# Four edits to the order of row gathers, neighbour lists and first-graph copies in a graph-network kernel on one core

## The chip, the core and the metric

The kernel runs on one core of one Trainium2 chip, in one launch. The core has five engines, each with its own instruction stream worked through in order: TensorE (PE in the profile, its weight loads PEld), VectorE (DVE), ScalarE (ACT), GpSimd (POOL) and SyncE (SP). SP here only issues DMAs; GpSimd mostly issues gathers by index, called indirect DMAs. The metric is the device time of the launch in microseconds (us), less is better.

## The reference

Sixteen graphs of 1024 nodes with 64 channels each, and a symmetric weighted adjacency matrix of 1024 x 1024 per graph. Four layers follow one another; each normalises the rows of x, applies a relu to give h, and adds a result to x:

```
layer 0: x += tanh([h, adj @ h] @ W1 + b1) @ W2 + b2
layer 1: x += ((adj + I) @ h) / rowsum(adj + I)
layer 2: x += relu((h + quantiles(h)) @ W1 + b1) @ W2 + b2, times the node mask
layer 3: x += (adj @ h / degree) @ Wn + h @ Ws + bias
```

The quantiles of layer 2 set the shape of the kernel. For each node the neighbours are those with a positive entry, thinned out by a rule on their rank (every k-th neighbour of a node with more than 10 is removed, in both directions), and the node itself. Over the remaining neighbours, channel by channel, the reference sorts the values of h and takes the 0.25, 0.5 and 0.75 quantiles with linear interpolation, weighted 0.25, 0.5, 0.25.

## The kernel before, in words

Nodes of a graph are dealt by falling number of neighbours to 8 blocks of 128, one node per partition. Blocks are sorted in five groups, `GROUPS`: block 0 alone, block 1 alone, and the pairs 2-3, 4-5, 6-7. `PLACES` says how many neighbours a block's nodes may have at most in its columns (21, 19, 17, 16, 15, 13, 12, 11), and `LISTS` how many are listed (40, 24, 24 and five times 16). The few nodes of block 0 with more than 21 neighbours have the surplus fetched as packed rows (`PACKS`).

Six Python generators (streams) each run over the graphs and emit the instructions of one kind of work:

- `adjacency`: loads the matrix two blocks at a time (`load_rows`, on SP), makes a 0/1 form `nb` (L947, VectorE), transposes by TensorE (L954) into `adjt` with PSUM copies on ScalarE (L955), finds removed neighbours `gone` (L978-L1011), writes per node a row of neighbour codes `keys_d` to DRAM (relu at L1032, a Sign for the count at L1035, both ScalarE), and ranks the nodes (L1055 to L1081).
- `layers`: layers 0 and 1 and the h of layer 2, stored to DRAM as `h_d` (L1236).
- `neighbour_lists`: per block one gather of key rows on GpSimd (`load_keys`, L1096, four buffers, so the load for block i+4 follows block i), then VectorE's MAX8 takes eight neighbours a round (L1111, L1125, L1127) into `found`. After the eighth block three operations turn all 168 columns into row numbers, `index` (L1135 to L1137). Then the numbers of the packed rows go to DRAM and back as `pack` through seven SP transfers (L1141, L1143), and the quantile weights are made.
- `gathers`: per graph three packed gathers (L1264), then group by group, place by place, one gather of 128 rows of `h_d` into `raw` per block (L1283), 124 in all. A group's `raw` has one buffer, so group k of graph b is emitted after the sort of group k of graph b-1. The packed rows travel through DRAM into `raw` by SP (L1273, L1276).
- `sorts`: compare-and-exchange steps on VectorE over `raw` and `other` (L1316) and the weighted sum (L1333, L1335).
- `tail`: gathers the results back by node (L1355), ends layer 2 and computes layer 3.

The order is set by a planner that runs while the program is built. Each stream yields the time at which it wants to go on, by a model clock `clk` (`clk.dve`, `clk.pool`, ...). The loop at the end of `direct_path` always takes the first stream in the list that is due, adjacency first, sorts last; when none is due, the clock jumps. `done` holds what has been emitted, and `over_graphs` holds a stream back until what it needs is there: gathers need `("index", b)` and `("layers", b)`. A gate (L919 to L925) ties GpSimd to this order: VectorE clears a mark, and GpSimd copies it before the gathers behind it, so they can't start before VectorE has come to this place. Gates stand at least 3 us of the model clock apart.

Of the kernel before, what the change touches and what calls it, by code (L numbers as in the profile page):

```python
# [7 lines left out]
F32 = mybir.dt.float32  # L8
F16 = mybir.dt.float16
BF = mybir.dt.bfloat16  # L10
I32 = mybir.dt.int32
U16 = mybir.dt.uint16
U8 = mybir.dt.uint8
AF = mybir.ActivationFunctionType
ALU = mybir.AluOpType
AX = mybir.AxisListType

P = 128
# [38 lines left out]
PACKS, NPACK = [(0, 0, 21, 2, 64), (1, 0, 23, 1, 32), (1, 32, 24, 4, 24), (2, 0, 28, 10, 12)], 3  # L57

LISTS = [40, 24, 24, 16, 16, 16, 16, 16]
KB = 4  # L60


# [669 lines left out]
def direct_path(ctx: ExitStack, tc: tile.TileContext, t: dict, out: bass.AP, flag):  # L732
# [207 lines left out]
    def adjacency(b):  # L940
# [4 lines left out]
        for i in range(NB):  # L945
            a = queued.pop(0)
            ts(nb[:, i, :], a, 0.0, None, op0=ALU.is_gt)  # L947
            d = slice(i * P, (i + 1) * P)
            tt(nb[:, i, d], nb[:, i, d], offdiag, ALU.mult)
            for q in range(2):  # L950
                p = bank()
                for u in range(4):
                    j = 4 * q + u
                    nc.tensor.transpose(p[:, u * P:(u + 1) * P], a[:, j * P:(j + 1) * P], identf)  # L954
                nc.scalar.copy(adjt[:, 4 * q:4 * q + 4, i * P:(i + 1) * P],  # L955
                               p.rearrange("p (u m) -> p u m", m=P))
            if i % 2:
                load_rows((NB * b + i) // 2 + 2)
            for q in range(2):
                s = slice(q * 512, (q + 1) * 512)  # L960
                act(nb[:, i, s], nb[:, i, s], AF.Copy, accum_out=mn[:, q, i:i + 1])  # L961
            yield max(after(0.9, pe=2.2, act=2.9) - 3.0, clk.dve + 3.1)
# [55 lines left out]
        for i in range(NB):  # L1018

            p = bank2()  # L1020
            for q in range(2):
                s = slice(q * 512, (q + 1) * 512)
                nc.tensor.matmul(p[:, s], big_i, nb[:, i, s], start=True, stop=False)
                nc.tensor.matmul(p[:, s], big_i, gone[:, i, s], start=False, stop=False)
                nc.tensor.matmul(p[:, s], onerow, jrow[:, s], start=False, stop=False)
                for j in range(4 * q, 4 * q + 4):
                    d = slice(j * P, (j + 1) * P)
                    nc.tensor.matmul(p[:, d], gone[:, j, i * P:(i + 1) * P], big_i, start=False,  # L1028
                                     stop=j == 4 * q + 3 and i // 4 != q)
                if i // 4 == q:  # L1030
                    nc.tensor.matmul(p[:, i * P:(i + 1) * P], identh, big_i, start=False, stop=True)
            act(nb[:, i, :], p, AF.Relu)  # L1032
            if i % 2:
                nc.sync.dma_start(keys_d[(i - 1) * P:(i + 1) * P].rearrange("(u p) n -> p u n", p=P), nb[:, i - 1:i + 1])
            act(p, p, AF.Sign, accum_out=ms[:, i:i + 1])  # L1035
            yield after(0, pe=4.5, act=2.3) - 4.0
# [50 lines left out]
    def neighbour_lists(b):  # L1087
# [13 lines left out]
        gate()  # L1101
        for i in range(KB):
            load_keys(i)
        total = sum(LISTS)
        found = lists.tile([P, total], F32, name="found", bufs=1)
        m = g["m"]
        o = 0
        for i in range(NB):
            src, at = ks[i]
            yield at  # L1110
            nc.vector.max(out=found[:, o:o + 8], in_=src)  # L1111
            clk.dve += 1.15
            yield clk.dve
            less, before = src.bitcast(I16), None
            for r in range(1, LISTS[i] // 8):


                least = found[:, o + 7:o + 8]
                if r == 1:
                    ts(less, src, least, None, op0=ALU.subtract)  # L1120
                else:
                    ts(less, less, before, least, op0=ALU.add, op1=ALU.subtract)
                before = least
                most = nodes.tile([P, 8], U16, name="most")
                nc.vector.max(out=most, in_=less.bitcast(U16))  # L1125
                o += 8
                ts(found[:, o:o + 8], most.bitcast(I16), 0.0, least, op0=ALU.min, op1=ALU.add)  # L1127
                clk.dve += 1.8
                yield clk.dve
            o += 8  # L1130
            load_keys(i + KB)
        index = lists.tile([P, total], I32, name="index")
        to, of = (v.rearrange("p (s u) -> p u s", u=2) for v in (index, found))
        none = lists.tile([P, total // 2], F32, tag="far", name="none", bufs=1)
        nc.vector.tensor_copy(to[:, 1], of[:, 1])  # L1135
        ts(none, of[:, 0], 0.0, float(N + 1), op0=ALU.is_equal, op1=ALU.mult)
        tt(to[:, 0], none, of[:, 0], ALU.add)  # L1137
        pack_d = dram.tile([NPACK, P], I32, name="pack_d")
        pack = nodes.tile([P, NPACK], I32, name="pack")
        for l, p0, s0, ns, nn in PACKS:  # L1140
            nc.sync.dma_start(pack_d[l, p0:p0 + ns * nn].rearrange("(n s) -> n s", s=ns), index[:nn, s0:s0 + ns])  # L1141
        for l, size in enumerate(sizes):
            nc.sync.dma_start(pack[:size, l:l + 1], pack_d[l, :size].rearrange("(n o) -> n o", o=1))  # L1143

        s = nodes.tile([P, 2, NB], F32, name="s")
        tt(s[:, 0], m, cap8, ALU.is_gt)
# [21 lines left out]
        act(far, far, AF.Abs)  # L1168
        for k, w in enumerate((0.25, 0.5, 0.25)):
            act(far[:, k], far[:, k], AF.Relu, bias=wcol[:, k:k + 1], scale=-w)  # L1170
        g.update(index=index, pack=pack)
        done.add(("index", b))
        yield after(1.7, act=1.7)
        while b >= 2 and ("sorts", b - 2) not in done:
            yield None
# [70 lines left out]

    def gathers(b):
        g = state[b]
        yield max(g["rows_at"], clk.pool)
        for k, (b0, n, cap, *_) in enumerate(GROUPS):  # L1250
            while not (b == 0 or ("sort", b - 1, k) in done):
                yield None
            raw = raws.tile([P, cap, n * C], F32, name=f"raw{k}")
            clk.pool = max(clk.pool, clk.dve)
            for i in range(n):
                for s in (PLACES[b0 + i], PLACES[b0 + i] + 1):
                    if s < cap:
                        z = raw[:, s:cap:2, i * C:(i + 1) * C]
                        nc.scalar.copy(z, none[:, s % 2:s % 2 + 1, None].to_broadcast([P, (cap - s + 1) // 2, C]))
                        clk.act = max(clk.act, clk.dve) + 0.2 + (cap - s + 1) // 2 * C / 1400  # L1260
            if k == 0:
                packed = nodes.tile([P, NPACK * C], F32, name="packed", bufs=1)
                for l, size in enumerate(sizes):
                    nc.gpsimd.indirect_dma_start(packed[:size, l * C:(l + 1) * C], None, h_ds[b % 3],  # L1264
                                                 bass.IndirectOffsetOnAxis(ap=g["pack"][:size, l:l + 1], axis=0))
                    clk.pool += 1.39
                rows_d = dram.tile([NPACK, P, C], F32, name="rows_d")
            for s in range(cap):
                if s % (4 // n) == 0:
                    gate()  # L1270
                if k == 0 and s == 9:
                    for l, size in enumerate(sizes):
                        nc.sync.dma_start(rows_d[l, :size], packed[:size, l * C:(l + 1) * C])  # L1273
                if k == 0 and s == 17:
                    for l, p0, s0, ns, nn in PACKS:
                        nc.sync.dma_start(raw[:nn, s0:s0 + ns, :],  # L1276
                                          rows_d[l, p0:p0 + ns * nn].rearrange("(n s) c -> n s c", s=ns))
                for i in range(n):
                    if s >= PLACES[b0 + i]:
                        continue  # L1280
                    clk.pool += 1.39
                    at = sum(LISTS[:b0 + i]) + s
                    nc.gpsimd.indirect_dma_start(raw[:, s, i * C:(i + 1) * C], None, h_ds[b % 3],  # L1283
                                                 bass.IndirectOffsetOnAxis(ap=g["index"][:, at:at + 1], axis=0))
                if (s + 1) % (4 // n) == 0:
                    yield clk.pool - 5
            g[f"raw{k}"] = (raw, clk.pool + 4)
            done.add(("gather", b, k))
        done.add(("gathers", b))
# [125 lines left out]
    nc.vector.memset(none[:, :1], BIG)  # L1415
    nc.vector.memset(none[:, 1:], 0.0)
    sizes = [max(p0 + ns * nn for l, p0, _, ns, nn in PACKS if l == k) for k in range(NPACK)]
    programs = [_program(*group[2:]) for group in GROUPS]
    edge = lists.tile([1, 2, C], F32, tag="ab", name="edge")
    nc.vector.memset(edge[:, 0], 0.0)  # L1420
# [6 lines left out]
    def over_graphs(step, *needs):  # L1427
# [7 lines left out]
        over_graphs(adjacency, ("adjt", 1), ("keys", 1), ("sorts", 3)),  # L1435
        over_graphs(layers, ("rows", 0), ("tail", 3)),
        over_graphs(tail, ("sorts", 0)),
        over_graphs(gathers, ("index", 0), ("layers", 0)),
        over_graphs(neighbour_lists, ("keys", 0), ("gathers", 2), ("sorts", 3)),
        over_graphs(sorts, ("lists", 0)),  # L1440
    ]
# [148 lines left out]
```

## Time and profile before

| what | value |
|---|---|
| median of 3 runs | 3667.72 us (3661.44 to 3670.98) |
| the profiled execution, its own time | 3892.48 us |
| its span, first to last instruction | 3890.7 us |
| granted TensorE clock in it | 0.679 |
| busy: VectorE / GpSimd / TensorE / ScalarE | 78% / 68% / 52% / 37% |
| row gathers L1283 | 1984, 1085 ns each, 532.6 us of issue gaps before them |

The profiled execution is slower than the runs without a profile, so durations from it add up to its own 3892 us and not to the median. A row of the profile names line, engine, operation and tiles (written<-read), the number of instructions, their busy time and mean duration, and after the second bar the engine's idle time before them with what ended it. "issue" is a gap for which the profile shows no cause; behind GpSimd's DMA instructions it is about 0.3 us each time. In a timeline the first two columns are start and duration in us.

### The profile page before, as it was taken

To read this page: it belongs to the slowest core of one execution; us is meant where nothing else is said; L and a number is where in the kernel's file an instruction comes from. 1 tells how busy PE (TensorE), PEld (TensorE's weight loads), DVE (VectorE), ACT (ScalarE), POOL (GpSimd) and SP (SyncE) were. 2 spreads that over 40 slices of the span, in tenths; PEclk is the share of its full clock that TensorE was granted. 3 is DMA by queue.
4 is the path that set the end of the run, shared out by engine and by line. 5 is a ranking of instruction groups with operands and counts; after the bars stand their busy time and mean duration, and the time that the engine had idled before them with its cause. 6 is when DMAs were issued, how large, how long until landed. Compare 5 with 4: busy or idle time off the path is not lost.

```text
span 3890.7 us, 30892 instructions
## 1 busy us (share of the span) xinstructions
PE 2010.3 (52%) x7587; PEld 934.0 (24%) x7587; DVE 3040.5 (78%) x7345; ACT 1424.2 (37%) x2786; POOL 2650.6 (68%) x2792
## 2 busy tenths in 40 slices
PE   6463463746554474645546565565457545641113
PEld 3222221223222222222222222232222212220101
DVE  2557877969787897888788798989699867979572
ACT  5444343244443434333342444343444424330000
POOL 1077565867767776776767677777778776777781
PEclk8676666667676686666666676767667666765555
DMA  2313233152423425233341525242343424232121
GB/s 89 124 40 117 48 98 114 47 166 53 153 64 94 121 65 152 69 114 79 86 126 48 172 54 163 58 156 56 100 119 108 113 52 126 65 105 59 43 52 55
DMA packets 237343, 362.37 MB, mean 93 GB/s; under 512 B 126848, under 2 KB 128496, under 8 KB 237152
## 3 DMA queue, kind: packets, MB, share of 16 engines
q1 hardware_dynamic: 156912, 255.00, 19.0%
q0 software_dynamic: 80096, 104.70, 13.5%
q8 instruction: 62, 1.02, 0.1%
q14 instruction: 129, 1.06, 0.1%
q10 hardware_dynamic: 144, 0.59, 0.0%
HBM read 245.30 MB, written 114.81 MB: 93 GB/s over the span
## 4 chain that ended last, share of the span: by engine, by line
DVE 42%; issue 16%; POOL 10%; PE 10%; another core or an unknown queue 9%; ACT 9%; DMA 4%; SPq 0%; DVEq 0%; ACTq 0%; POOLq 0%
DVE other L1316 11%; DVE raw L1316 10%; POOL raw L1283 8%; DVE most L1125 5%; PE pt L882 4%; DVE found L1111 2%; DVE agg L1335 2%; ACT adjt L1220 2%; ACT sink L1055 2%; DVE k L1120 1%; DMA k<-keys_d,node 1%; POOL res L1355 1%; PE pt L906 1%; DVE nb L947 1%
## 5 line engine op out<-in xcount | busy, mean ns | idle before, releaser
L1283 POOL DMA_INDIRECT raw<-h_d,index x1984 | 2151.8, 1085 | 558.9 <-issue 532.6
L1316 DVE TENSOR_TENSOR other<-raw 128x512 f32<-128x512 f32 (+11 forms) x816 | 536.8, 688 | 152.0 <-DMA raw<-h_d,index 103.6
L882 PE MATMUL pt<-adjt,ha 128*65 128x512 f32 (+1 forms) x1024 | 489.7, 640 | 63.0 <-DVE ha L1207 27.1
L924 POOL COPY gate<-mark 1x1 f32<-1x1 f32 x477 | 162.7, 341 | 409.4 <-DVE mark L922 372.6
L994 PE MATMUL pt<-eh,nbt 128*128 128x512 f16 (+3 forms) x1024 | 238.3, 381 | 322.1 <-ACT nbt L983 256.1
L954 PE MATMUL pt<-ef,a 128*128 128x128 f32 x1024 | 212.5, 367 | 294.9 <-issue 112.4
L1316 DVE TENSOR_TENSOR raw<-other 128x512 f32<-128x512 f32 (+10 forms) x464 | 355.8, 791 | 5.3
L1125 DVE MAX8 most<-k 128x8 uint16<-128x1024 uint16 x208 | 255.4, 1228 | 10.9 <-DVE k L1120 3.3
L954 PEld LDWEIGHTS pt<-ef,a 128*128 128x128 f32 x1024 | 163.4, 190 | 383.8 <-issue 186.6
L1032 ACT ACTIVATE nb<-pt 128x1024 f16<-128x1024 f32 x128 | 130.6, 1021 | 328.7 <-remote 169.3
L955 ACT COPY adjt<-pt 128x512 f32<-128x512 f32 x256 | 140.3, 585 | 282.6 <-remote 148.0
L882 PEld LDWEIGHTS pt<-adjt,ha 128*65 128x65 f32 (+1 forms) x1024 | 149.2, 149 | 386.3 <-issue 375.3
L1028 PE MATMUL pt<-eh,gone 128*128 128x128 f16 x1024 | 128.7, 255 | 181.9 <-DVE gone L1006 90.6
L1316 DVE TENSOR_TENSOR raw<-other,raw 128x640 f32<-128x640 f32 (+3 forms) x448 | 216.5, 494 | 6.7 <-remote 1.8
L994 PEld LDWEIGHTS <-nbt 128*128 128x128 f16 x1024 | 111.2, 121 | 452.8 <-ACT nbt L983 286.0
L1316 DVE TENSOR_TENSOR raw<-raw,other 128x128 f32<-128x128 f32 (+7 forms) x496 | 211.6, 436 | 6.1
L883 ACT COPY big<-pt 64x1024 f32<-64x1024 f32 (+1 forms) x32 | 32.2, 1008 | 502.5 <-PE pt L882 299.3
L961 ACT ACTIVATE nb<-nb 128x512 f16<-128x512 f16 x256 | 159.7, 629 | 147.7 <-DVE nb L947 53.8
L1392 PE MATMUL tm<-at,ha 128*64 128x512 f32 x512 | 176.8, 794 | 67.0 <-DMA at<-adjt_d 59.1
L1316 DVE TENSOR_TENSOR other<-other,raw 128x128 f32<-128x128 f32 (+4 forms) x448 | 201.6, 461 | 4.5 <-DVE other L1316 0.3
L1001 ACT ACTIVATE gone<-pt,sf 128x512 f16<-128x512 f32 x256 | 161.6, 685 | 104.7 <-remote 35.1
L1111 DVE MAX8 found<-k 128x8 f32<-128x1024 f16 x128 | 156.4, 1222 | 42.5 <-DMA k<-keys_d,node 42.4
(189 smaller groups left out, 4249.3 us busy)
## 6 DMA issues: line engine op xcount, KB each, us to landing
a<-in_adj_dram SPq DMA_DIRECT2D x64, 1024.0 KB
adjt_d<-adjt SPq DMA_DIRECT2D x64, 1024.0 KB
at<-adjt_d SPq DMA_DIRECT2D x128, 512.0 KB
keys_d<-nb SPq DMA_DIRECT2D x64, 512.0 KB
raw<-h_d,index POOLq DMA_INDIRECT x1984
x<-in_x_dram SPq DMA_DIRECT2D x16, 256.0 KB
h_d<-h SPq DMA_DIRECT2D x16, 256.0 KB
agg_d<-agg SPq DMA_DIRECT2D x16, 256.0 KB
```

Of the source, the lines that this page charges most:

```text
L882: nc.tensor.matmul(p[p0:p0 + n, s], h[:, j, :n], adjt[:, j, s], start=j == 0, stop=j == NB - 1)
L924: nc.gpsimd.tensor_copy(opened[:, k % 2:k % 2 + 1], slots[:, k % 8:k % 8 + 1])
L954: nc.tensor.transpose(p[:, u * P:(u + 1) * P], a[:, j * P:(j + 1) * P], identf)
L955: nc.scalar.copy(adjt[:, 4 * q:4 * q + 4, i * P:(i + 1) * P], p.rearrange("p (u m) -> p u m", m=P))
L961: act(nb[:, i, s], nb[:, i, s], AF.Copy, accum_out=mn[:, q, i:i + 1])
L994: nc.tensor.matmul(p[:, o:e], nbt[:, j, :], stair[:, :e - o], start=j % 4 == 0, stop=j % 4 == 3 and j != i)
L1001: act(gone[:, i, s], p[:, s], AF.Abs, bias=sf[:, 2 + q, i:i + 1], scale=2.0)
L1111: nc.vector.max(out=found[:, o:o + 8], in_=src)
L1125: nc.vector.max(out=most, in_=less.bitcast(U16))
L1283: nc.gpsimd.indirect_dma_start(raw[:, s, i * C:(i + 1) * C], None, h_ds[b % 3], bass.IndirectOffsetOnAxis(ap=g["index"][:, at:at + 1], axi ...
L1316: tt(view(two[to], *((i, vi) if greater else (j, vj)), w), view(two[s], i, vi, w), view(two[u], j, vj, w), ALU.max if greater else ALU.min)
L1392: nc.tensor.matmul(p[q * C:(q + 1) * C, :], ha[:, j, :], even(ats[j], q), start=j == 0, stop=j == NB - 1)
```

## The change

Block by block, the change does this:

- `found` becomes one constant tile of 176 columns, cleared once, for all graphs. The lists of paired blocks are interleaved in it column by column (`FIRST` has the first column of each group), so that one view covers the group.
- As soon as the last block of a group has its list, three operations make that group's row numbers, and `("index", b, k)` is set; the three at the end go. `gathers` waits for group k's numbers before group k, no longer for all of them.
- The packed numbers go to DRAM and back after block 0 instead of after block 7. The packed gathers move from before the first place to place 4, their way out to DRAM from place 9 to 11.
- `gathers` sets no gate at places past the last gathered one (only group 0 has a whole stretch of those, 21 to 37).
- In graph 0 the second PSUM copy of each block's transposes (128x512) and the relu of L1032 (128x1024) run on VectorE; in the other graphs they stay on ScalarE.

```diff
--- before.py
+++ after.py
@@ -57,6 +57,7 @@
 PACKS, NPACK = [(0, 0, 21, 2, 64), (1, 0, 23, 1, 32), (1, 32, 24, 4, 24), (2, 0, 28, 10, 12)], 3
 
 LISTS = [40, 24, 24, 16, 16, 16, 16, 16]
+FIRST = [0, 40, 64, 112, 144, 176]
 KB = 4
 
 
@@ -952,8 +953,8 @@
                 for u in range(4):
                     j = 4 * q + u
                     nc.tensor.transpose(p[:, u * P:(u + 1) * P], a[:, j * P:(j + 1) * P], identf)
-                nc.scalar.copy(adjt[:, 4 * q:4 * q + 4, i * P:(i + 1) * P],
-                               p.rearrange("p (u m) -> p u m", m=P))
+                copy = nc.vector.tensor_copy if b == 0 and q else nc.scalar.copy
+                copy(adjt[:, 4 * q:4 * q + 4, i * P:(i + 1) * P], p.rearrange("p (u m) -> p u m", m=P))
             if i % 2:
                 load_rows((NB * b + i) // 2 + 2)
             for q in range(2):
@@ -1029,7 +1030,10 @@
                                      stop=j == 4 * q + 3 and i // 4 != q)
                 if i // 4 == q:
                     nc.tensor.matmul(p[:, i * P:(i + 1) * P], identh, big_i, start=False, stop=True)
-            act(nb[:, i, :], p, AF.Relu)
+            if b:
+                act(nb[:, i, :], p, AF.Relu)
+            else:
+                ts(nb[:, i, :], p, 0.0, None, op0=ALU.max)
             if i % 2:
                 nc.sync.dma_start(keys_d[(i - 1) * P:(i + 1) * P].rearrange("(u p) n -> p u n", p=P), nb[:, i - 1:i + 1])
             act(p, p, AF.Sign, accum_out=ms[:, i:i + 1])
@@ -1101,21 +1105,25 @@
         gate()
         for i in range(KB):
             load_keys(i)
-        total = sum(LISTS)
-        found = lists.tile([P, total], F32, name="found", bufs=1)
+        index = lists.tile([P, FIRST[-1]], I32, name="index")
+        pack_d = dram.tile([NPACK, P], I32, name="pack_d")
+        pack = nodes.tile([P, NPACK], I32, name="pack")
+        g.update(index=index, pack=pack)
         m = g["m"]
-        o = 0
         for i in range(NB):
             src, at = ks[i]
+            k, n = next((k, n) for k, (b0, n, *_) in enumerate(GROUPS) if b0 <= i < b0 + n)
+            first = FIRST[k] + (i - GROUPS[k][0])
+            eights = [found[:, e:e + 7 * n + 1:n] for e in range(first, first + LISTS[i] * n, 8 * n)]
             yield at
-            nc.vector.max(out=found[:, o:o + 8], in_=src)
+            nc.vector.max(out=eights[0], in_=src)
             clk.dve += 1.15
             yield clk.dve
             less, before = src.bitcast(I16), None
             for r in range(1, LISTS[i] // 8):
 
 
-                least = found[:, o + 7:o + 8]
+                least = eights[r - 1][:, 7:8]
                 if r == 1:
                     ts(less, src, least, None, op0=ALU.subtract)
                 else:
@@ -1123,24 +1131,26 @@
                 before = least
                 most = nodes.tile([P, 8], U16, name="most")
                 nc.vector.max(out=most, in_=less.bitcast(U16))
-                o += 8
-                ts(found[:, o:o + 8], most.bitcast(I16), 0.0, least, op0=ALU.min, op1=ALU.add)
+                ts(eights[r], most.bitcast(I16), 0.0, least, op0=ALU.min, op1=ALU.add)
                 clk.dve += 1.8
                 yield clk.dve
-            o += 8
             load_keys(i + KB)
-        index = lists.tile([P, total], I32, name="index")
-        to, of = (v.rearrange("p (s u) -> p u s", u=2) for v in (index, found))
-        none = lists.tile([P, total // 2], F32, tag="far", name="none", bufs=1)
-        nc.vector.tensor_copy(to[:, 1], of[:, 1])
-        ts(none, of[:, 0], 0.0, float(N + 1), op0=ALU.is_equal, op1=ALU.mult)
-        tt(to[:, 0], none, of[:, 0], ALU.add)
-        pack_d = dram.tile([NPACK, P], I32, name="pack_d")
-        pack = nodes.tile([P, NPACK], I32, name="pack")
-        for l, p0, s0, ns, nn in PACKS:
-            nc.sync.dma_start(pack_d[l, p0:p0 + ns * nn].rearrange("(n s) -> n s", s=ns), index[:nn, s0:s0 + ns])
-        for l, size in enumerate(sizes):
-            nc.sync.dma_start(pack[:size, l:l + 1], pack_d[l, :size].rearrange("(n o) -> n o", o=1))
+            if i + 1 == GROUPS[k][0] + n:
+                e, z = FIRST[k], FIRST[k + 1]
+                to, of = (v[:, e:z].rearrange("p (s u i) -> p u s i", u=2, i=n) for v in (index, found))
+                less = nodes.tile([P, 32], F32, name="less", bufs=1)[:, :(z - e) // 2]
+                less = less.rearrange("p (s i) -> p s i", i=n)
+                ts(less, of[:, 0], 0.0, float(N + 1), op0=ALU.is_equal, op1=ALU.mult)
+                nc.vector.tensor_copy(to[:, 1], of[:, 1])
+                tt(to[:, 0], less, of[:, 0], ALU.add)
+                clk.dve += 0.5
+                done.add(("index", b, k))
+            if i == 0:
+                for l, p0, s0, ns, nn in PACKS:
+                    nc.sync.dma_start(pack_d[l, p0:p0 + ns * nn].rearrange("(n s) -> n s", s=ns),
+                                      index[:nn, s0:s0 + ns])
+                for l, size in enumerate(sizes):
+                    nc.sync.dma_start(pack[:size, l:l + 1], pack_d[l, :size].rearrange("(n o) -> n o", o=1))
 
         s = nodes.tile([P, 2, NB], F32, name="s")
         tt(s[:, 0], m, cap8, ALU.is_gt)
@@ -1168,8 +1178,6 @@
         act(far, far, AF.Abs)
         for k, w in enumerate((0.25, 0.5, 0.25)):
             act(far[:, k], far[:, k], AF.Relu, bias=wcol[:, k:k + 1], scale=-w)
-        g.update(index=index, pack=pack)
-        done.add(("index", b))
         yield after(1.7, act=1.7)
         while b >= 2 and ("sorts", b - 2) not in done:
             yield None
@@ -1246,9 +1254,11 @@
 
     def gathers(b):
         g = state[b]
+        while ("index", b, 0) not in done:
+            yield None
         yield max(g["rows_at"], clk.pool)
         for k, (b0, n, cap, *_) in enumerate(GROUPS):
-            while not (b == 0 or ("sort", b - 1, k) in done):
+            while ("index", b, k) not in done or not (b == 0 or ("sort", b - 1, k) in done):
                 yield None
             raw = raws.tile([P, cap, n * C], F32, name=f"raw{k}")
             clk.pool = max(clk.pool, clk.dve)
@@ -1260,15 +1270,16 @@
                         clk.act = max(clk.act, clk.dve) + 0.2 + (cap - s + 1) // 2 * C / 1400
             if k == 0:
                 packed = nodes.tile([P, NPACK * C], F32, name="packed", bufs=1)
-                for l, size in enumerate(sizes):
-                    nc.gpsimd.indirect_dma_start(packed[:size, l * C:(l + 1) * C], None, h_ds[b % 3],
-                                                 bass.IndirectOffsetOnAxis(ap=g["pack"][:size, l:l + 1], axis=0))
-                    clk.pool += 1.39
                 rows_d = dram.tile([NPACK, P, C], F32, name="rows_d")
             for s in range(cap):
-                if s % (4 // n) == 0:
+                if s % (4 // n) == 0 and s < PLACES[b0]:
                     gate()
-                if k == 0 and s == 9:
+                if k == 0 and s == 4:
+                    for l, size in enumerate(sizes):
+                        nc.gpsimd.indirect_dma_start(packed[:size, l * C:(l + 1) * C], None, h_ds[b % 3],
+                                                     bass.IndirectOffsetOnAxis(ap=g["pack"][:size, l:l + 1], axis=0))
+                        clk.pool += 1.39
+                if k == 0 and s == 11:
                     for l, size in enumerate(sizes):
                         nc.sync.dma_start(rows_d[l, :size], packed[:size, l * C:(l + 1) * C])
                 if k == 0 and s == 17:
@@ -1279,7 +1290,7 @@
                     if s >= PLACES[b0 + i]:
                         continue
                     clk.pool += 1.39
-                    at = sum(LISTS[:b0 + i]) + s
+                    at = FIRST[k] + s * n + i
                     nc.gpsimd.indirect_dma_start(raw[:, s, i * C:(i + 1) * C], None, h_ds[b % 3],
                                                  bass.IndirectOffsetOnAxis(ap=g["index"][:, at:at + 1], axis=0))
                 if (s + 1) % (4 // n) == 0:
@@ -1415,6 +1426,8 @@
     nc.vector.memset(none[:, :1], BIG)
     nc.vector.memset(none[:, 1:], 0.0)
     sizes = [max(p0 + ns * nn for l, p0, _, ns, nn in PACKS if l == k) for k in range(NPACK)]
+    found = const.tile([P, FIRST[-1]], F32, name="found")
+    nc.vector.memset(found, 0.0)
     programs = [_program(*group[2:]) for group in GROUPS]
     edge = lists.tile([1, 2, C], F32, tag="ab", name="edge")
     nc.vector.memset(edge[:, 0], 0.0)
@@ -1435,7 +1448,7 @@
         over_graphs(adjacency, ("adjt", 1), ("keys", 1), ("sorts", 3)),
         over_graphs(layers, ("rows", 0), ("tail", 3)),
         over_graphs(tail, ("sorts", 0)),
-        over_graphs(gathers, ("index", 0), ("layers", 0)),
+        over_graphs(gathers, ("layers", 0)),
         over_graphs(neighbour_lists, ("keys", 0), ("gathers", 2), ("sorts", 3)),
         over_graphs(sorts, ("lists", 0)),
     ]
```

## Prediction

> **What bounds the kernel now.** I began with the busy times and the rows by line. No engine is full: VectorE is busy 78% and GpSimd 68%. But GpSimd's rows have an "issue" gap behind nearly every instruction, which belongs to its work:
>
> ```profile
> PE 2010.3 (52%) x7587; PEld 934.0 (24%) x7587; DVE 3040.5 (78%) x7345; ACT 1424.2 (37%) x2786; POOL 2650.6 (68%) x2792
> ...
> L1283 POOL DMA_INDIRECT raw<-h_d,index x1984 | 2151.8, 1085 | 558.9 <-issue 532.6 <-DVE mark L922 10.0 <-DVE raw L1316 4.7
> L924 POOL COPY gate<-mark 1x1 f32<-1x1 f32 x477 | 162.7, 341 | 409.4 <-DVE mark L922 372.6 <-issue 8.9 <-DVE raw L1316 7.1
> ```
>
> A row gather costs 1.085 + 0.28 = 1.37 us. A graph issues 124 of them, 3 packed, 8 of keys and 8 of results: 143 x 1.37 = 196 us, with some 10 us of gate copies 206.
>
> Then I followed GpSimd in the timeline: the first packed gather of each graph starts at 197.0, 426.1, 668.0, 894.6, 1110.7, 1341.7, 1570.2, 1807.2, 2037.9 and, for the last, 3601.3 us; the last gather ends at 3802, and 88 us of the last graph's sort and tail follow. So the span is 197 us of filling, 16 turns of 225 us on GpSimd, and the tail. From graph 5 on, a graph's first gather follows the previous graph's last one at once; for graphs 0 to 3 GpSimd stands idle before it:
>
> ```profile
> 173.88 1.41 POOL L1096 DMA_INDIRECT k<-keys_d,node  x1 [2.23 <-DVE found L1127]
> 196.96 0.95 POOL L1264 DMA_INDIRECT packed<-h_d,pack  x1 [21.67 <-DMA pack<-pack_d]
> ...
> 397.72 0.95 POOL L1096 DMA_INDIRECT k<-keys_d,node  x1 [0.30 <-issue]
> 426.06 0.95 POOL L1264 DMA_INDIRECT packed<-h_d,pack  x1 [27.39 <-DMA pack<-pack_d]
> ```
>
> What it waits for is seen on VectorE: block 0's list is done at 158.66, but the lists of seven more blocks come before the conversion to row numbers:
>
> ```profile
> 158.43 0.23 DVE L1127 TENSOR_SCALAR found<-most,found 128x8 f32<-128x8 int16 x1
> 158.57 1.22 DVE L1111 MAX8 found<-k 128x8 f32<-128x1024 f16 x1
> ...
> 188.23 0.21 DVE L1135 CAST index<-found 128x84 int32<-128x84 f32 x1
> 188.35 0.20 DVE L1136 TENSOR_SCALAR none<-found 128x84 f32<-128x84 f32 x1
> 188.58 0.25 DVE L1137 TENSOR_TENSOR index<-none,found 128x84 int32<-128x84 f32 x1
> 188.74 0.16 DVE L1146 TENSOR_TENSOR s<-m,ef 128x8 f32<-128x8 f32 x1
> ```
>
> After 188.8 the four numbers-to-DRAM and three back transfers take 8.1 us, and GpSimd, in order, has three packed gathers at its head. Last, the stretches: in the steady part VectorE has 16% idle, so it is near a second bound:
>
> ```profile
> 1575.00:3603.00 2028.00, 1098.46 (x4120) 505.77 (x4119) 1710.58 (x4129) 764.34 (x1490) 1492.87 (x1554) 0.68 0.35 97
> ```
>
> [...]
>
> **Earlier first gather.** With numbers by group, the first gather needs block 0's list, three small conversions, and the rows h_d. I read the end of block 0's list (fourth L1127 of a graph) for each graph and let GpSimd begin at that plus 1.0 us, or when it is free, whichever is later; a graph's turn keeps its present length (200, 230, 222, 216, 231, 228, 237, 231 us for graphs 0 to 7, from its first packed gather until GpSimd is free). Each turn still holds eight key loads.
> Graph 0: 158.7 + 1 = 159.7 against 197.0, 37 us sooner; it ends at 360.
> Graph 1: list at 380.7, start 381.7 against 426.1, 44 sooner; ends at 612.
> Graph 2: list at 610.3, GpSimd free at 612: 56 sooner.
> Graph 3: list at 838.2, 839.2 against 894.6: 55 sooner.
> Graph 4: list at 1059.2, 1060.2 against 1110.7: 50 sooner.
> Graph 5: list at 1288.8, GpSimd free at 1291: 51 sooner.
> Graphs 6, 7: GpSimd is free at 1519 and 1756, after the lists (1508.5, 1731.3): 51 sooner.
> Graph 8: the rows bind: h_d is stored at 1986.4, lands some 4 us later: 1991 against 2037.9, **47 sooner**.
> After that no list or row comes later than the shifted gathers (graph 15: list 3472.8, rows stored 3506, start 3554), so 47 us stay to the end. In this the lists keep their times: they follow the adjacency chain, one graph behind another every 220 us, which the gathers don't release. What is late next is that chain itself (list of graph 5) and the layers (rows of graph 8).
>
> **Packed gathers later.** The seven transfers on SP's queue are now issued behind block 0 and needed four row gathers (5.5 us), the fifth key load (1.3) and a gate on: some 7.5 us against 8.1. But on SP, in order, they now stand among the adjacency loads of the next graph, which wait there for a free buffer (four between 145 and 180 us, 11.5 us the longest such wait), where before they came after them. What stands behind them on SP waits the less. I charge 3 us once, since only the last graph whose start the list sets passes it on; bounds 0 and 12. Their rows go out at place 11 instead of 9 and back at 17 as before: 8 us of cover for a 4 us hop; cost nothing. If that cover goes, the sort of group 0 waits (it did once, 11.4 us).
>
> **More conversions.** Three operations become fifteen of 12 to 24 elements. The three now take 0.51 us (188.23 to 188.74). Operations of 8 elements beside them take 0.17 and start 0.08 (independent) or 0.20 (dependent) apart, so a group costs 0.42, five 2.1: 1.6 us more a graph, 26 us in all. The strided results of MAX and the one memset of found (well under 1 us) I put at nothing. VectorE's 16% idle can hide all of it, bound 0; through the gates, where GpSimd waits for VectorE's place (372.6 us in the run), all of it could come through, bound 26. I take half, 13.
>
> **Gates at empty places.** Up to four gates in group 0 go. The timeline shows such a gate between the 21st and 22nd row gather in 3 of 16 graphs, so: nothing, at most 3 us and a little.
>
> **First graph.** Eight copies of 128x512 leave ScalarE (start to start 0.53 us) for VectorE (0.69 for the same shape from PSUM, L1229). ScalarE works without a gap from 16.9 to 35.5 us at 2.2 us a block there, VectorE waits for the adjacency DMA meanwhile; 8 x 0.53 = 4.3 off ScalarE, of which I take 3.5, as TensorE and the DMA are close behind; worst, VectorE's copy waits for TensorE with the next block's comparison behind it: 3 us lost. The eight Relu of 128x1024 (0.92 each on ScalarE) become VectorE operations[...] and Sign on the same PSUM tile must follow them instead of following on its own engine: TensorE's 2.2 us a block already sets that pace; nothing, bounds 5 either way.
>
> **Sum**: -47 + 3 + 13 - 3.5 = -34.5 us on the profiled execution's 3892.5: 3858. That execution is slower than the runs, whose median is 3667.7 (0.942 of it); scaling, -32.5: about **3635 us**. Bounds: -47 - 4.3 - 5 - 3 = -59 (3612) and -47 + 12 + 26 + 3 + 5 = -1 (3667).
>
> **Rivals.** *VectorE is the true bound* (0.12): gates follow its order, so earlier gathers only wait at their gates. For it: 372.6 us of gate waits. Against: 124 of them are the wait for the start, and in the steady part, graph after graph, sorts begin some 4 us after their gathers and end before the next ones need them. Then only graph 0's fill is kept, 37 scaled, less the 26: about 3657, or 3667 if nothing is kept.
> *Key loads queue behind row gathers* (0.14), the slower side. Loads 5 to 8 of a graph now stand on GpSimd's queue behind gathers that the planner lets run 5 us ahead; VectorE, in order, then waits at MAX8 L1111, and the adjacency chain waits behind it. Now that wait is 42.4 us in nine cases. It decides from 3 us more a graph (48 us). With 6 more, 1.5 for each late load, it is 96 us: 3892 + 60 = 3952, scaled 3724. Against it: in graphs 5 to 15 these loads already lie among the previous graph's gathers, and four buffers cover it.
> *Nothing released* (0.04): another wait (layers, sort of the graph before) holds the first gathers, and only 0 to 26 us are added: 3668 to 3692. Against: the rows of graphs 0 and 1 are stored at 139 and 348 us, ahead of block 0's lists at 158.7 and 380.7.
> The forecast has 0.70. About 0.3% is what a measurement of this kernel can tell from no change: 3656.7 to 3678.7. Faster takes the forecast's whole and a third of the first rival, 0.74; same 0.11; slower 0.15. The range reaches below the bound for an order that falls well, and above into the slower rivals: 3590 to 3690.
>
> **What would show it.** Right: first row gather at about 157 to 160, 382 and 612; packed gathers fifth to seventh in a graph, with waits for pack under 3 us each; the last graph's first gather some 45 us sooner and 88 us from the last gather to the end; 240 conversion operations adding some 26 us to VectorE's busy time. Wrong: gate waits larger by the shift (first rival); MAX8 L1111 waiting over 90 us for keys, lists drawn out (second); first gathers where they were (third).

## The result, and the profile after

The changed kernel takes 3633.7 us (median of 4 runs, 3631.7 to 3640.4) against 3666.9 of the kernel before: ratio 0.9909, 95% interval 0.9894 to 0.9924, some 33 us less. The forecast was 3635 us.

One thing has to be known to read the profiles. The first profile of the kernel before was 3890.7 us long; on the chip of the first experiments the same kernel was profiled again, and this execution took 3667.3 us (span 3665.4) where the other runs on that chip took 3653 to 3666. So it is not the profiling that made the first one long. The kernel before had medians of 3661, 3838 and 3895 us on the three chips of the experiments; the first profile most likely comes from a chip like the last of these, though its chip is not on record. So ratios are compared on one chip only, and the changed kernel's profile (3638.5 us) is laid beside the second profile of the kernel before, called "before, again". That the two are from one chip is not on record either; the changed kernel's profiled execution was the slowest of its four.

Busy times of the changed kernel, from its page:

```profile
PE 1993.7 (55%) x7587; PEld 923.9 (25%) x7587; DVE 3072.9 (84%) x7539; ACT 1410.6 (39%) x2770; POOL 2651.7 (73%) x2777
...
L1294 POOL DMA_INDIRECT raw<-h_d,index x1984 | 2165.2, 1091 | 558.8 <-issue 498.8
L925 POOL COPY gate<-mark 1x1 f32<-1x1 f32 x462 | 156.4, 339 | 225.0 <-DVE mark L923 217.3
```

GpSimd's work is what it was: 1984 row gathers of 1.09 us. VectorE has 194 instructions more: 192 conversions and 16 help operations, less 15 marks, and one memset. What moved is the start. GpSimd's timeline of the kernel before, again, at the first gathers of graphs 0 and 1 (start, duration, instruction, and in brackets the idle time ahead of it):

```profile
200.32 0.94 POOL L1264 DMA_INDIRECT packed<-h_d,pack  x1 [21.15 <-DMA pack<-pack_d]
...
412.20 0.94 POOL L1264 DMA_INDIRECT packed<-h_d,pack  x1 [24.52 <-DMA pack<-pack_d]
```

The same places in the changed kernel:

```profile
163.26 0.94 POOL L1100 DMA_INDIRECT k<-keys_d,node  x1 [9.73 <-DVE found L1134]
165.76 0.35 POOL L925 COPY gate<-mark 1x1 f32<-1x1 f32 x1 [1.56 <-DVE mark L923]
166.45 0.97 POOL L1294 DMA_INDIRECT raw<-h_d,index  x1 [0.34 <-issue]
...
359.28 1.41 POOL L1100 DMA_INDIRECT k<-keys_d,node  x1 [0.72 <-DVE most L1133]
361.73 0.40 POOL L925 COPY gate<-mark 1x1 f32<-1x1 f32 x1 [1.04 <-DVE mark L923]
362.62 0.97 POOL L1294 DMA_INDIRECT raw<-h_d,index  x1 [0.49 <-ACT raw L1269]
```

The waits of 21 and 24 us are gone: row gathers follow the fifth key load and a gate. A small wait is left at that gate, where GpSimd waits for VectorE to come to its mark: it is up to 6.4 us ahead of a graph's first row gather, 45 us over the sixteen graphs, against 11 in before, again. Starts of the first gather, read from both timelines:

| graph | before, again | changed | sooner | forecast |
|---|---|---|---|---|
| 0 | 200.3 | 166.5 | 34 | 37 |
| 1 | 412.2 | 362.6 | 50 | 44 |
| 2 | 627 | 579 | 48 | 56 |
| 3 | 838 | 793 | 45 | 55 |
| 5 | 1265 | 1216 | 49 | 51 |
| 8 | 1905 | 1860 | 45 | 47 |
| 15 | 3385 | 3358 | 27 | 47 |

### The profile page after: what moved, and what is told of

Same layout as the page of the kernel before. It is cut to its first block, busy times and chain, and to the rows that moved or that the text cites. A ratio compares the mean times of both kernels' runs of the same rounds, so it can differ in the third digit from the quotient of the medians.

```text
span 3638.5 us, 31082 instructions
## 1 busy us (share of the span) xinstructions
PE 1993.7 (55%) x7587; PEld 923.9 (25%) x7587; DVE 3072.9 (84%) x7539; ACT 1410.6 (39%) x2770; POOL 2651.7 (73%) x2777
## 4 chain that ended last, share of the span: by engine, by line
DVE 61%; POOL 11%; issue 11%; DMA 7%; PE 5%; ACT 3%; SPq 0%; DVEq 0%; POOLq 0%; ACTq 0%
DVE raw L1327 16%; DVE other L1327 16%; POOL raw L1294 10%; DVE most L1133 6%; PE pt L883 4%; DVE found L1119 4%; DMA raw<-h_d,index 3%; DVE agg L1346 2%; ACT adjt L1228 2%; DMA k<-keys_d,node 2%; DVE k L1128 2%; DVE nb L948 2%; DVE found L1134 1%; DVE k L1130 1%; DVE gone L1007 1%
## 5 line engine op out<-in xcount | busy, mean ns | idle before, releaser
L955 PE MATMUL pt<-ef,a 128*128 128x128 f32 x1024 | 205.2, 356 | 220.2 <-ACT adjt L957 136.2
L955 PEld LDWEIGHTS pt<-ef,a 128*128 128x128 f32 x1024 | 155.6, 183 | 321.6 <-ACT adjt L957 173.9
L1403 PE MATMUL tm<-at,ha 128*64 128x512 f32 x512 | 175.3, 786 | 74.5 <-DMA at<-adjt_d 74.5
L1119 DVE MAX8 found<-k 128x8 f32<-128x1024 f16 x128 | 156.3, 1221 | 51.6 <-DMA k<-keys_d,node 51.6
L891 PE MATMUL pt<-ef,res 128*128 128x128 f32 x128 | 38.9, 399 | 291.9 <-DMA res<-agg_d,pos 291.9
L1034 ACT ACTIVATE nb<-pt 128x1024 f16<-128x1024 f32 x120 | 122.4, 1020 | 164.9 <-PE pt L1032 89.2
```

The costliest lines, as they stand in the source:

```text
L1119: nc.vector.max(out=eights[0], in_=src)
L1403: nc.tensor.matmul(p[q * C:(q + 1) * C, :], ha[:, j, :], even(ats[j], q), start=j == 0, stop=j == NB - 1)
```

## The experiments

**The kernel before, profiled again.**

> The kernel before, unchanged, profiled once more, because its profiled execution of 3892 us lies 6% above its own runs and the one of the changed kernel (3640 us) does not. Theory A (the gain is the earlier first gather, everything in the profile before was stretched alike): span about 3665 us; the first packed gathers of graphs 0 to 3 again with GpSimd idle 5 to 25 us before them, each some 40 to 50 us after the end of block 0's list; the last graph's first gather some 35 us later than in the changed kernel (3358 us). Theory B (the old profile showed a wait that the runs don't have): no idle time on GpSimd before the first gathers of graphs 1 to 3, and the difference to the changed kernel spread over the turns of all graphs.

Its span is 3665.4 us, GpSimd is idle 21.2, 24.5, 11.3 and 3.7 us before the first gathers of graphs 0 to 3, and the last graph starts 27 us later than in the changed kernel, where 35 was expected. Theory A holds. The waits view of GpSimd, old profile first, then again:

```profile
POOL gate L924 <- DVE mark L922: 372.6, 59, 124.2
```

```profile
POOL gate L924 <- DVE mark L922: 202.8, 54, 128.3
```

Columns are total us, times, longest. The longest is the wait for the program's start. The rest, 248 against 74.5 us, makes up 174 of the 225 us between the two spans: on GpSimd the longer execution shows mostly as waits at its gates.

**The early start taken back.** Gathers wait for the last group's numbers:

```diff
-        while ("index", b, 0) not in done:
+        while ("index", b, len(GROUPS) - 1) not in done:
```

> The changed kernel, but a graph's gathers wait for the numbers of its last group instead of the first. All else as changed: fifteen conversions, packed numbers sent after block 0, VectorE's help in graph 0. Theory A (the gain is the earlier first gather): it comes back to the time before or a little above, 3660 to 3685 us, first row gather of graph 0 near 203 us. Theory B (the gain lies elsewhere: front, packed rows or gates): stays within 10 us of the changed kernel, 3625 to 3645.

Measured: 3668.4 us, ratio 1.0023 (1.0016 to 1.0030). The gain is gone and a little more, as theory A has it. GpSimd's timeline shows the wait back, in the gate now instead of at the packed rows:

```profile
181.69 1.41 POOL L1100 DMA_INDIRECT k<-keys_d,node  x1 [2.23 <-DVE most L1133]
202.17 0.36 POOL L925 COPY gate<-mark 1x1 f32<-1x1 f32 x1 [19.08 <-DVE mark L923]
202.86 1.31 POOL L1294 DMA_INDIRECT raw<-h_d,index  x1 [0.33 <-issue]
```

Beside packed_first below, on the same chip at 3627.4 us, the early start is worth some 41 us (the two differ in the packed gathers' place as well).

**Packed gathers first again.**

```diff
-                if k == 0 and s == 4:
+                if k == 0 and s == 0:
...
-                if k == 0 and s == 11:
+                if k == 0 and s == 9:
```

> The changed kernel with the packed gathers at the head of a graph again (place 0) and their rows sent out at place 9; the packed numbers still go to DRAM after block 0. If GpSimd is the bound at the first gathers, it now waits for the packed numbers with all row gathers behind: in graph 0 some 6 us (8 us of two hops less what passes anyway), in later graphs only where block 0's list is less than some 8 us ahead of GpSimd. The changed kernel's trace has block 0's lists 3 to 10 us ahead in graphs 1 to 4 and 20 or more from graph 5 on, so the loss is that of graphs 0 to 2, in sum some 6 to 12 us: 3640 to 3646. Rival (packed rows were always covered): no change, 3632 to 3636.

Measured: 3627.4 us, ratio 0.9911 (0.9897 to 0.9926); the changed kernel has 0.9909, which would be 3628 us on this chip. The rival is nearer. The wait is there, GpSimd is idle 5.7, 9.3 and 6.0 us before the first gathers of graphs 0 to 2, but no loss shows in the time. In the changed kernel the packed rows are not free either: in its waits view they cost 12.1 us in five waits for `pack`, which is the same kind of loss.

**No help from VectorE in graph 0.**

```diff
-                copy = nc.vector.tensor_copy if b == 0 and q else nc.scalar.copy
+                copy = nc.scalar.copy
...
-            if b:
-                act(nb[:, i, :], p, AF.Relu)
-            else:
-                ts(nb[:, i, :], p, 0.0, None, op0=ALU.max)
+            act(nb[:, i, :], p, AF.Relu)
```

> The changed kernel with ScalarE doing all copies and relus of graph 0 as before. My step took 3.5 us from the copies and nothing from the relus: 3637 us, bounds 3630 to 3642. A rival reading of the changed kernel's trace, where graph 0's keys were ready at 147 us against 142 in the kernel before, is that the help costs time: then 3626 to 3631, keys of graph 0 ready earlier than 147 us.

Measured: 3620.6 us (4 runs, 3619.6 to 3623.7), ratio 0.9893 (0.9878 to 0.9908). The help doesn't pay; that it costs is not shown by the times, since the interval overlaps the changed kernel's. The profiles show what it does. Keys of graph 0 are ready, that is, the operation that writes `node`, the row numbers for the key loads, is done, at 140 us instead of 147; the changed kernel first, then without the help:

```profile
146.58 0.17 DVE L1085 CAST node<-pt 128x8 int32<-128x8 f32 x1 [0.65 <-ACT m L1082]
```

```profile
140.02 0.17 DVE L1082 CAST node<-pt 128x8 int32<-128x8 f32 x1 [0.65 <-ACT m L1079]
```

The last graph starts 47 us sooner than in the kernel before, again, just the forecast shift. The two halves of the help were tried apart next. Here is VectorE's timeline of the changed kernel in graph 0:

```profile
112.23 1.22 DVE L1036 TENSOR_SCALAR nb<-pt 128x1024 f16<-128x1024 f32 x1 [19.86 <-PE pt L1032]
121.05 1.22 DVE L1036 TENSOR_SCALAR nb<-pt 128x1024 f16<-128x1024 f32 x1 [7.59 <-PE pt L1032]
122.19 0.20 DVE L1235 RECIPROCAL den<-pt 128x8 f32<-128x8 f32 x1
...
127.32 1.23 DVE L1036 TENSOR_SCALAR nb<-pt 128x1024 f16<-128x1024 f32 x1 [1.03 <-PE pt L1032]
```

and without the help:

```profile
109.38 0.21 DVE L1232 RECIPROCAL den<-pt 128x8 f32<-128x8 f32 x1 [23.04 <-PE pt L1219]
...
112.79 0.69 DVE L856 TENSOR_TENSOR mid<-x,stat 128x512 f32<-128x512 f32 x1
```

The reciprocal opens layer 1's run of VectorE operations, 109.4 to 113.5 us. With the help it stands behind a relu that waits for TensorE, and starts at 122.2. TensorE in turn waits for its two PSUM tiles, which ScalarE's Sign (behind its own pass over the adjacency, 107.4 to 115.8 us) and these same layer 1 operations hold. The waits view of TensorE, 80 to 131 us of the changed kernel, shows both:

```profile
PE pt L1024 <- ACT pt L1039: 5.3, 3, 4.7
...
PE pt L1024 <- DVE mid L1237: 2.2, 1, 2.2
```

Without the help the second isn't there. So the last relu stands behind layer 1 and ends at 128.5 us instead of 122.0.

**The two halves of the help**, on a second chip (before: 3837.5 us), with the changed kernel beside them: `copies_only` takes back the relus, `relu_only` the copies.

> The changed kernel, unchanged, so that it stands on one chip beside its own parts. Expected the measured ratio again, 0.9894 to 0.9924 of the kernel before.

> The changed kernel with the relus of graph 0 back on ScalarE; only the eight copies stay on VectorE. Theory: the copies gain what the traces show, end of graph 0's copies near 32.4 us against 34.2, some 2 us; the relus on VectorE are what costs, since they stand in VectorE's order behind layer 1's operations while TensorE needs their PSUM tile. Then this one is the fastest of the parts, 2 us under the version with all on ScalarE and 6 to 12 us under the changed kernel: ratio 0.987 to 0.990, the last relu of graph 0 at about 121 us and not 128. Rival (the version with all on ScalarE was fast because TensorE's clock stayed up in its first 110 us): ratio as the changed kernel's.

> The changed kernel with the copies of graph 0 back on ScalarE; only the eight relus are on VectorE. Theory (the relus cost): as slow as the changed kernel or 2 us slower, ratio 0.991 to 0.993, TensorE waiting 2 to 5 us for VectorE twice between 110 and 125 us in graph 0. Rival (TensorE's clock): as the version with all on ScalarE, 0.9878 to 0.9908.

Measured: changed kernel 0.9801 (0.9761 to 0.9841), outside the interval expected for it on its low side: it gains 69 us here (3837.5 to 3768.9), twice what it gained in the first measurement, and no run shows why. copies_only 0.9776 (0.9734 to 0.9819); relu_only 0.9816 (0.9768 to 0.9864). On this chip runs scatter too much for the ratios to tell the halves apart. The traces do. Graph 0's copies end at 32.1 us in copies_only and 34.1 in relu_only; its last relu at 121.2 and 130.2; its keys are ready at 139.4 and 148.5. Over all profiles, keys with the relus on VectorE are ready at 146 to 149 us (six), with them on ScalarE at 139 to 142 (six) or 146 (two). Those two are before, again and conversions_twice. In both, the stretch from 82 to 108 us has a granted TensorE clock of 0.80; of before, again (stretch, its length, busy us and instructions of PE, PEld, DVE, ACT and POOL, clock, DMA share, GB/s):

```profile
82.00:108.00 26.00, 24.69 (x90) 8.67 (x90) 2.60 (x8) 12.75 (x19) 0.00 (x0) 0.80 0.11 41
```

In the changed kernel, copies_only and relu_only that stretch has a clock of 1.00, so a lower clock goes with the two late ones, but not with the relus' delay. That speaks against the rival. The copies end 2 us sooner, but the keys don't: relu_only has them at 148.5, the changed kernel beside it, with the copies on VectorE too, at 149.1. The relus make the keys later by 6 to 10 us within one chip. What of this reaches the end of the kernel the times don't settle.

**Gates at the empty places**, same chip:

```diff
-                if s % (4 // n) == 0 and s < PLACES[b0]:
+                if s % (4 // n) == 0:
```

> The changed kernel with gates at the empty places of group 0 as well. I put them at nothing, at most 3 us: ratio within 0.001 of the changed kernel's. Rival (each removed gate spared a wait for VectorE at the end of group 0's gathers): up to 16 gates more in the trace and 8 to 15 us slower, ratio 0.993 to 0.996.

Measured: 0.9835 (0.9786 to 0.9885), 3770.9 us against the changed kernel's 3768.9 there. The trace has 462 gates in both, and the same instructions on every engine: the planner's 3 us keep the added places from setting any. So this is the changed kernel measured twice, and the difference of the two ratios is the chip's scatter. It also means that this edit of the change did nothing: the 15 gates fewer than in the kernel before come from the rest of the change.

**The rest of the change alone**, on a third chip (before: 3894.9 us): late start and no help.

> The changed kernel without VectorE's help in graph 0 and with a graph's gathers waiting for its last group's numbers: what is left of the change is the fifteen conversions instead of three, the interleaved lists, the packed rows' new places and the missing gates. My sum charged the conversions 13 us and the packed rows 3: ratio 1.003 to 1.005. Rival (VectorE's idle time hides the conversions, and late_start's 1.0023 was the relus): ratio 0.9985 to 1.001.

Measured: 1.0172 (1.0121 to 1.0224), outside both. What is left of the change doesn't gain, but the conversions can't be read off it: waits at gates are 526.0 us here, of a span of 3943.8, and the emission order differs from the kernel before's. Beside copies_again below, on the same chip, it is 103 us slower (3950.6 against 3847.7). The two differ only in the late start and in eight copies of graph 0, so the early start is worth far more here than the 41 us of the first chip; the waits at gates differ by 130 us (526.0 against 396.5). Why was not found.

**Copies only, again, on the third chip**, as the base for the next two.

> The same as copies_only (relus of graph 0 on ScalarE, copies on VectorE), beside the next two on one chip. Theory (the relus cost some 9 us, the copies gain 2): about 0.988 to 0.9895 of the kernel before on a chip that runs that one at some 3662 us, and 3614 to 3622 us; if the relus cost nothing, 3628 to 3634.

Measured: 0.9900 (0.9869 to 0.9932), just above the expected ratio, which lies inside the interval; the times expected for a fast chip have no counterpart.

**Conversions twice.**

```diff
                 tt(to[:, 0], less, of[:, 0], ALU.add)
+                more = nodes.tile([P, 64], I32, name="more", bufs=1)[:, :z - e]
+                more = more.rearrange("p (s u i) -> p u s i", u=2, i=n)
+                ts(less, of[:, 0], 0.0, float(N + 1), op0=ALU.is_equal, op1=ALU.mult)
+                nc.vector.tensor_copy(more[:, 1], of[:, 1])
+                tt(more[:, 0], less, of[:, 0], ALU.add)
```

> copies_again with every conversion of a group followed by the same three operations into an unused tile, at no cost in the planner's clock, so that the order stays: 240 operations more, some 33 us of VectorE. My sum let half of such an addition through: 13 to 17 us slower than copies_again. Rival (the conversions are hidden): within 3 us of it. If VectorE is the true bound: 26 to 33 us slower.

Measured: 3867.6 against 3847.7 us, ratios 0.9941 (0.9917 to 0.9966) and 0.9900. VectorE's busy time grows by 31.5 us (3067.9 to 3099.4), the time by some 16 to 20. By the medians somewhat over half comes through, near what the sum had; the intervals overlap, so neither rival is excluded.

**Wide gates.**

```diff
-        if not marks or clk.dve > marks[-1] + 3.0:
+        if not marks or clk.dve > marks[-1] + 8.0:
```

> copies_again with gates at least 8 us of the planner's clock apart instead of 3. A gate takes 0.34 us on GpSimd and some 0.16 us of gap. If GpSimd's own work is the bound from the first graph on, as the turns without idle time say, a third to a half of the 462 gates left saves some 250 x 0.4 = 100 us on GpSimd at most, and as VectorE is 84% busy some of it turns into waits: 20 to 80 us faster than copies_again. Rival (the gates' waits only stand for VectorE's lag, and the gathers wait the same without them): within 10 us; or slower, when gathers ahead of their place take a buffer or a queue too early.

Measured: 1.0285 (1.0231 to 1.0340), 154 us slower than copies_again. The theory falls. GpSimd's busy time does shrink, by 90 us (2633.4 to 2543.3), but the waits at gates grow by 159; copies_again first, then wide gates, in the waits view of GpSimd:

```profile
POOL gate L925 <- DVE mark L923: 396.5, 72, 124.2
```

```profile
POOL gate L925 <- DVE mark L923: 555.8, 66, 123.0
```

With 264 gates instead of 462 GpSimd waits longer at nearly as many of them. Why VectorE comes to the marks later (it waits 114.1 us for ScalarE's squares instead of 48.6) was not tried. Nor is it shown that the gates are what costs: TensorE stands idle without a shown cause (last section) for 479.2 us here and 349.8 in copies_again, which is 129 of the 154 us.

No version was shown to beat the changed kernel beyond its interval. The two candidates keep the relus of graph 0 on ScalarE: 0.9893 without any help, 0.9776 with the copies alone, each on its own chip.

## Why the prediction was right, and where a step was not

- **Earlier first gather: right in kind and size, for the reason given.** In the table above the shift is 34 to 50 us up to graph 8 where 37 to 56 was worked out. Taking the early start back took the gain back. The idle gaps were nearly the same in the long first profile (21.7 and 27.4 us) as in the second (21.2 and 24.5), so the shift needed no scaling between these two; on the slower chips the change, or its early start, was worth more than the gaps (69 and 103 us), which the prediction has no term for.
- **"47 us stay to the end": not in the changed kernel's profile.** From graph 8 to 15 the shift shrinks from 45 to 27. GpSimd's gate waits without the first are 88 us in the changed kernel and 74.5 in the kernel before, again: 14 us more, at VectorE. This is the first rival's mechanism, on a part of the shift. How much of the shrinking is the kernel's and how much this one execution's is open: the two profiled executions are 27 us apart where the medians are 33, and on the chip of before, again, packed_first has 41 left and the version without the help 47.
- **"The lists keep their times" and "the rows bind at graph 8": wrong.** Both streams moved along. Block 0's list of graph 5 is done at 1194 us instead of 1217 (before, again), and the rows of graph 8 are stored at 1807, 53 us ahead of its first gather. So neither is late next; from graph 1 on it is GpSimd itself, with a few us for VectorE at the gate. Little hung on it: 4 us of the working.
- **Packed gathers, +3: about nothing.** The wait exists (at most 3.3 us at a time) and putting them first costs no more.
- **Conversions, +13: not refuted.** 192 added operations put 21 us on VectorE (3037.6 to 3058.8 in the build without help) where 26 were estimated; of a second such set some half came through by the medians, with a wide interval. The row of 8-element operations was a good price, 0.17 us: the 80 final ones, of 12 to 24 elements, have a median of 177 ns.
- **Gates: nothing, as said**, with the same 462 when the code for them is put back.
- **First graph, -3.5: wrong, and by the traces of the other sign.** The copies end 2 us sooner, but at the keys nothing of it is seen. The relus' term, put at nothing by comparing paces, with TensorE's 2.2 us a block as the slower (a relu takes 1.22 us on VectorE), makes graph 0's keys 6 to 10 us later: the step looked at the engine pairs on the PSUM tile, and not at what else stands in VectorE's order there. The sentence that Sign must wait was right; that layer 1 then waits behind the relus was missing.
- **Key loads behind row gathers (the second rival): not seen.** Its sign was a wait for keys of over 90 us at the first MAX8. The changed kernel has 51.6 us, before, again 46.0:

```profile
L1119 DVE MAX8 found<-k 128x8 f32<-128x1024 f16 x128 | 156.3, 1221 | 51.6 <-DMA k<-keys_d,node 51.6
```

So the mechanism is right, and that -34.5 came so near is partly luck: in the profiles the shift lost more on the way to the end, the conversions perhaps cost less, the front has the other sign. On the second chip the same forecast would have been half of what was measured.

## What to carry to other kernels

Where one engine works without a gap through the whole program, look for the first thing that it waits for and split the producer, so that the first piece releases it; where the kernel before took some 3660 us the gain, 33 us, paid once, was a part of the 61 us that GpSimd stood idle ahead of its first four turns (21.2, 24.5, 11.3 and 3.7), and on the slower chips it was more (69 us for the change, 103 for the early start). An operation given to an idle engine is not free if other work is queued behind it there: here the reciprocal of layer 1 started at 122.2 us instead of 109.4, behind a relu that waited for TensorE, and the keys came 6 to 10 us later. Read what stands behind the new wait. A gate or semaphore wait on the busiest engine is a place to read how far the others lag; in the one trial here, taking 198 of 462 such gates away didn't take the lag away (waits of 555.8 us instead of 396.5).

## What the runs showed of the hardware that was not expected

One kernel took 3661, 3838 and 3895 us on three chips. Two profiles of it, 3890.7 and 3665.4 us long, have almost the same busy times of VectorE and GpSimd: 3040.5 and 3037.6 us on VectorE, 2650.6 and 2644.8 on GpSimd, at a granted TensorE clock of 0.68 and 0.70. What differs is TensorE. In the long profile it stands idle 80 times, 300.8 us in all and up to 21.9 us at a time, for no cause that the profile shows; these are the two largest groups:

```profile
PE pt L954 <- issue: 112.4, 30, 17.3
PE pt L994 <- issue: 63.4, 12, 21.9
```

The short profile has no such wait. Nor has any of the five profiles with spans of 3618 to 3665 us, whatever the version of the kernel; each of the nine of 3748 us and more has 77 to 125 of them, 233 to 479 us in all. In the long profile ScalarE waits longer too: 282.6 against 57.7 us ahead of the copies L955, and 328.7 against 170.9 ahead of the relus L1032. Whether TensorE really stands still there, or works longer than the profile's modelled ends say, and why, stays open.
